# Layer 0 of a four-layer kernel: an outer level of 26 products for blocks of 4 by 4 by 2 in place of 7 for 2 by 2 by 2

## The chip, the cores and the metric

One core of one Trainium2 chip. The metric is the device time of one launch in microseconds, the median of several runs. Engines are named as in the profile: PE (TensorE, matmuls), PEld (its weight loads), DVE (VectorE), ACT (ScalarE), POOL (GpSimd) and SP (SyncE, here a queue of DMAs). POOL also issues DMAs, among them all that add to what lies in memory.

## What is computed

The input x has 1024 images of 16 by 16 by 16 values, in float32. Four layers follow, each `x = x + layer(norm(x))` with a group norm over 8 groups. Layers 1 and 3 are cellular-automaton steps (two depthwise convolutions, a dense layer to 128, a dense layer to 16, a mask), layer 2 is a 3 by 3 convolution. This case is about layer 0, cut here to what matters:

```python
def _tt_matvec(vector, cores):        # cores: (1,16,16,16), (16,16,16,16), (16,16,16,1)
    res, bs = vector[:, None], vector.shape[0]
    for core in cores:
        r, o, i, k = core.shape
        res_t = res.reshape(bs, r, i, -1)
        new = jnp.einsum('roik,brix->bkox', core, res_t)
        ...
x = x + _tt_matvec(_gn(x), (core0, core1, core2))
```

So layer 0 is one matrix of 4096 by 4096, given by three small cores, times a matrix of 4096 by 1024 (the images as columns).

## The kernel before

Layer 0 is worked as a dense product with two levels of Strassen's scheme. The outer level cuts the matrix in 2 by 2 blocks and the images in two chunks of 512 (`xf[0]`, `xf[1]`): 7 products (the table `OUTER`) take the place of 8. The inner level (`INNER`) does the same for each of these products, with 256 images at a time. One outer product is a phase. A phase has 8 units (output lines `q` of 4, `w` of 2), a unit 7 inner products of 8 matmuls of 128x128 by 128x256 (`pieces`, L1299), in 14 pieces of 4 matmuls. Each inner product sums its 8 matmuls in half a PSUM bank; `gather` (L1337, L1343, L1345, L1347) adds the bank to the result tile `r` of the unit.

The weights are never stored whole. `train_setup` makes g, the product of the last two cores, and puts it in `g_dram`. For each unit `gload` (L1216) brings two tiles of g from there, and `build` (L1229, copied out by L1231) multiplies them with `R`, the small matrix of the first core with the signs of this outer product, made by `coefs`. `R` mixes two rows of lines of g, so a build makes the weights of any combination of the outer blocks that lie in those rows. `mix` (L1256, L1258) adds the blocks for the inner products on DVE.

The operand of a phase is 4096/2 rows by 512 images and lies in one of two big tiles `XN[p % 2]`. While a phase runs, `part_steps` loads the next operand's blocks into the other (L1059), with a second block by pieces of 512 KB in the work buffers `t4` (L1084) that are added (L1095), and `combined` (L1039) makes three more sums. `centre_scale` (L1010) applies the norm to a block at its first use; the normed block is kept in memory (`xb`). `store` (L1281, L1283) sends the finished `r` of a unit to one or two blocks of `xf`: the first time by a plain DMA of SP, and then by an accumulating DMA of POOL (512 KB each). The work buffers are `r` with two and `t4` with three buffers; three PSUM banks hold products (`o`), four the builds (`w`), one other things (`m`).

The order on each engine is written out by hand. `run(layer, us, loads, *spans)` emits the pieces of a phase one after the other, and between them other steps: each span is a list of steps with costs, spread over a part of the phase. So beside phase 0 lie the second half of the first chunk's input (transposes, L925) and the weight folds of layer 1 (`make1`; PE L390, POOL DMAs L402); beside phase 1 the input of the second chunk (loads by POOL, L907, statistics on DVE, L919, transposes); beside phase 2 the folds of layer 3; beside phases 3 and 4 the residual (16 accumulating DMAs for each chunk, L1141); at the start of phase 4 the conv weights of layer 2 (POOL DMAs L438, L446, L449); beside phase 6 the norm for layer 1.

The diff's functions and the loops that call them:

Of the kernel before, what the change touches and what calls it, by code (L numbers as in the profile page):

```python
# [2 lines left out]

# [17 lines left out]
P = 128  # L21
# [83 lines left out]
def conv_preact_kernel(ctx: ExitStack, tc: tile.TileContext, a: dict, out: bass.AP):  # L105
# [99 lines left out]
    al_d = cst("al_d", [P, 1])  # L205
    V.tensor_tensor(al_d, al_c[:, 0:1], al_c[:, 1:2], ALU.subtract)
# [16 lines left out]
    def nca_weights(pre, room):  # L223
# [7 lines left out]
        flat = room.rearrange("p n b -> p (n b)")  # L231

        def tmp(rows, line, lo, n):
            return flat[0:rows, NB * line + lo : NB * line + lo + n]

        fc0n, fc1n = tmp(HID, 0, 0, 48), tmp(16, 0, 64, HID)
        ones, cb, b0 = tmp(16, 0, 192, 48), tmp(48, 0, 240, 1), tmp(HID, 0, 241, 1)
        fc0t, fcb = tmp(16, 1, 0, 3 * HID), tmp(48, 2, 0, 3 * HID)
        ind = tmp(48, 3, 0, 768).rearrange("p (s r) -> p s r", s=3)

        fs = tmp(P, 5, 0, NB)
        tk4 = tmp(P, 6, 0, 32 * len(TERMS)).rearrange("p (n c) -> p n c", c=32)

        tc3 = tmp(96, 2, 384, 96).rearrange("p (j k) -> p j k", k=3)
        tk = tmp(96, 9, 0, 32 * len(TERMS)).rearrange("p (n c) -> p n c", c=32)
        tp = tmp(P, 14, 0, 72 * len(TERMS)).rearrange("p (n f m) -> p n f m", f=2, m=36)
        pk = tmp(P, 10, 0, 833)
        fold_e = [tmp(P, line, 0, 2 * NB) for line in (12, 7, 3)]
        zero = tmp(32, 0, 256, HID)
# [171 lines left out]
    def conv_weights():  # L421
# [44 lines left out]
    g_dram = dram.tile([2, 4, P, 2, 4, P], F32, tag="g_dram", name="g_dram")  # L466

    xb = {
        (b, n): dram.tile([P, S, NB], F32, tag=f"xb{b}{n}", name=f"xb{b}{n}")
        for b in range(2)  # L470
# [4 lines left out]
        ([(0, 0, 1)], {(1, 0): 1, (1, 1): -1}),  # L475
        ([(1, 0, 1), (0, 0, -1)], {(0, 0): 1, (1, 0): 1}),
        ([(1, 1, 1)], {(0, 1): 1, (0, 0): -1}),
        ([(0, 0, 1), (1, 1, 1)], {(0, 0): 1, (1, 1): 1}),
        ([(1, 0, 1), (1, 1, 1)], {(0, 0): 1}),
        ([(0, 1, 1), (1, 1, -1)], {(0, 1): 1, (1, 1): 1}),  # L480
        ([(0, 0, 1), (0, 1, 1)], {(1, 1): 1}),
    ]
    INNER = [
# [16 lines left out]
    def part_lines(p):  # L500
# [3 lines left out]
    mr = [  # L504
        XN[n].rearrange("p n b -> p (n b)")[:, 14336:15360].rearrange("p (k i) -> p k i", k=2)
        for n in range(NCH)
    ]
# [5 lines left out]
    def train_setup(room, kept_room):  # L513
# [4 lines left out]
        c1t = kept_room.rearrange("p (h x m) -> p h x m", h=2, x=4)  # L518
# [25 lines left out]
        def sums():  # L544

            t = st0["A"] = work([P, 3, P], "A", "A")
            pt = bank([P, 2, P], "o", "pc0")
            for e in range(2):
                T.transpose(pt[:, e], c0r[:, e].rearrange("p n k -> p (n k)"), ident)
            pt = pt.rearrange("p e (o b i) -> p b i e o", b=2, i=8)  # L550
            for b in range(2):
                A.copy(t[:, b].rearrange("p (i e o) -> p i e o", e=2, o=8), pt[:, b])
            V.tensor_tensor(t[:, 2], t[:, 0], t[:, 1], ALU.add)

        def cores():
# [4 lines left out]
            for h in range(2):  # L560
                pt = bank([P, 4, P], "o", "pc1")
                for x in range(4):
                    T.transpose(pt[:, x], c1s[:, h, x].rearrange("p r k -> p (r k)"), ident)
                A.copy(c1t[:, h], pt)

        def gmul(pg, h, ih, x, r, q):
            rows = slice(32 * r, 32 * r + 16)
            T.matmul(
                pg, c1t[rows, h, 2 * ih + x], c2[rows, 64 * q : 64 * q + 64], start=True, stop=True
            )  # L570

        def early():
# [3 lines left out]
            for x in range(2):  # L576
                for hi in range(4):
                    for r in range(4):
                        gmul(pg[r][:, x, hi], hi // 2, hi % 2, x, r, 0)
# [7 lines left out]
            for h in (1, 0):  # L587
                G.dma_start(
                    g_dram[h, 0].rearrange("p i o f -> p i (o f)"),
                    g[:, 2 * h : 2 * h + 2].rearrange("p i o f -> p i (o f)"),  # L590
                )

        def piece(q, h, r0):
# [20 lines left out]

        rest = [
            (0.6, lambda q=q, h=h, r0=r0: piece(q, h, r0))
            for q in range(1, 4) for h in range(2) for r0 in (0, 2)
        ]
        return sums, cores, early, rest

# [273 lines left out]
    def input_steps(n, tag, queue):  # L897
# [4 lines left out]
        slots = XN[1 - n].rearrange("p n b -> p (n b)").rearrange("p (s f) -> p s f", s=8)  # L902
        X = part_lines(0)

        def load(half, bg):
            b0 = n * NB + bg * P
            queue.dma_start(  # L907
                slots[:, 4 * half + bg],
# [3 lines left out]
        def stats(half, bg):  # L912
# [4 lines left out]
            x = slots[:, 4 * half + bg].rearrange("p (q g i) -> p q g i", g=8, i=2)  # L917
# [3 lines left out]
        def turn(h, wh):  # L921
            pt = bank([P, 4, P], tag[0], "ptin")
            for bg in range(4):
                x = slots[:, 4 * (h // 8) + bg].rearrange("p (h w f) -> p h w f", h=8, w=2)
                T.transpose(pt[:, bg], x[:, h % 8, wh], ident)  # L925
            pt = pt.rearrange("p g b -> p (g b)")
            if n == 0 and h < 8:
                if h >= 4:
                    A.copy(X[:, 1, 4 * wh + h - 4], pt)
                else:  # L930
                    A.copy(raw[:, 4 * wh + h], pt.rearrange("p (n i) -> p n i", n=2))
# [46 lines left out]
        def kept(b):  # L978
            for wh in range(2):
                to = xr[n][wh, 4 * b : 4 * b + 4]  # L980
                if b:
                    G.dma_start(to.rearrange("h p b -> p h b"), X[:, 1, 4 * wh : 4 * wh + 4])
                    continue
                for i in range(2):
                    G.dma_start(
                        to.rearrange("h p (n b) -> p h n b", n=2)[:, :, i],
                        raw[:, 4 * wh : 4 * wh + 4, i],
                    )
# [7 lines left out]
                for b in (2 * half, 2 * half + 1)  # L996
                for wh in range(2)
                for h in range(4 * b, 4 * b + 4)
# [44 lines left out]
    def raw_piece(b, n, l, k):  # L1043

        return xr[n][l // 4 % 2, 8 * b + 4 * (l // 8) + l % 4 : 8 * b + 4 * (l // 8) + l % 4 + k].rearrange(
            "h p b -> p h b"
        )

    full = slice(0, NB)

    def part_steps(p):


        blocks = OUTER[p][0]
        L = part_lines(p).rearrange("p b t i -> p (b t) i")
        b, n, _ = blocks[0]
        fresh = (b, n) not in made
        steps = [
            (0, lambda l=l: nc.sync.dma_start(  # L1059
                L[:, l : l + 4], raw_piece(b, n, l, 4) if fresh else xb[b, n][:, l : l + 4]  # L1060
            ))
            for l in range(0, 16, 4)
        ] + [8]
        if fresh:
            made.add((b, n))
            for l in range(0, 16, 2):
                x = L[:, l : l + 2]
                steps += [(1.2, lambda x=x, k=k: centre_scale(x, x, n, full, k)) for k in range(2)]
                if l % 4 == 2:
                    steps.append((0, lambda l=l: nc.sync.dma_start(  # L1070
                        xb[b, n][:, l - 2 : l + 2], L[:, l - 2 : l + 2]
                    )))
        if p == 1:
            return steps + from_first() + combined(p)
        if len(blocks) > 1:
            b1, n1, sign = blocks[1]
            fresh1 = (b1, n1) not in made
            made.add((b1, n1))
            t = {}

            def fetch(l):
                if l < 16:
# [841 lines left out]
```

## Time and profile before

| what | value |
|---|---|
| median of 3 runs | 2842.35 us (2841.89 to 2847.46) |
| the profiled execution | 2848.94 us, span 2847.2 us |
| granted PE clock, mean | 0.987 |
| PE busy | 2781.9 us, 98% |
| DVE, ACT, POOL busy | 1666.2, 1232.6, 452.2 us |
| layer 0 (40 to 1650 us): PE, DVE, ACT, POOL busy | 1597.22, 795.99, 419.15, 294.46 us |
| product matmuls of layer 0 (L1299) | 6272 records, 1426.3 us |
| builds (L1229) | 3584 records, 137.2 us |
| accumulating stores of `r` (L1283, from r and neg) | 64 |

How to read it: a float32 matmul has two records. "Busy" is the time in which at least one instruction of the engine runs; the matmuls overlap in the pipeline, so that a record of 384 ns takes 227 ns of busy time on average. The windows view gives the busy time by stretches, the chain of waits what ended last, and a wait in the timeline stands in brackets with what ended it.

### The profile page before, as it was taken

The page shows a single profiled execution, that of the slowest core. Times are in us where ns is not written, and L with a number is a line of the kernel's source. Part 1 is how long each engine was busy: PE and PEld are TensorE (multiplying, and loading weights), DVE is VectorE, ACT ScalarE, POOL GpSimd, SP SyncE. Part 2 cuts the span into 40 slices and gives each one's busy share as a digit, 9 for nine tenths or more (in the row PEclk, how much of TensorE's full clock was granted, in tenths as well). Part 3 has the DMA queues.
Part 4 walks back from the last instruction along what each step waited for, and adds up shares of the span by engine and source line. Part 5 has one row for each costly group of instructions (what it writes and reads, how often), then busy time and mean ns, then how long its engine had stood idle before and what let it go on. Part 6 is the DMA issues. An engine that isn't in the chain of part 4 may idle for free.

```text
span 2847.2 us, 47308 instructions
## 1 busy us (share of the span) xinstructions
PE 2781.9 (98%) x19028; PEld 1827.0 (64%) x19028; DVE 1666.2 (59%) x2196; ACT 1232.6 (43%) x2168; POOL 452.2 (16%) x661
## 2 busy tenths in 40 slices
PE   7999999999999999999999999999999999999997
PEld 5878888877888888888888843333333333334343
DVE  8426645633544345434456668757877877766654
ACT  3352232233221111211222256676778666666664
POOL 2351000263012131001000001101112221110000
PEclk7999999999999999999999999999999999999998
DMA  6276636366486477363261145546566866444665
GB/s 232 85 163 216 229 114 175 80 107 162 115 202 117 99 153 175 67 173 62 55 172 34 27 140 114 107 108 165 111 147 137 206 100 184 102 93 105 178 174 203
DMA packets 250188, 383.41 MB, mean 135 GB/s; under 512 B 30293, under 2 KB 140425, under 8 KB 243825
## 3 DMA queue, kind: packets, MB, share of 16 engines
q1 hardware_dynamic: 187344, 262.36, 28.7%
q0 software_dynamic: 62432, 117.88, 25.5%
q8 instruction: 151, 2.47, 0.4%
q14 instruction: 69, 0.56, 0.1%
q10 hardware_dynamic: 192, 0.13, 0.0%
HBM read 211.31 MB, written 173.92 MB: 135 GB/s over the span
## 4 chain that ended last, share of the span: by engine, by line
PE 73%; DVE 4%; issue 3%; DMA 2%; POOL 1%; ACT 1%; SPq 0%; DVEq 0%; POOLq 0%; ACTq 0%
PE po L1299 37%; PE ph L1708 17%; PE po L1537 7%; PE po L1392 5%; PE pw L1229 3%; PE po L1401 1%; DMA xn<-xf 1%; PE ptx L1601 1%; DVE xn L677 1%; DVE u L1549 1%; DMA convn<-in_L_conv_filters_dram 0%; PE pcnt L1577 0%; PE L_conv_pe L390 0%; PE pr L824 0%; DMA xf<-r 0%
## 5 line engine op out<-in xcount | busy, mean ns | idle before, releaser
L1299 PE MATMUL po<-xn,s 128*128 128x256 f32 x3584 | 815.3, 384 | 6.5 <-ACT r L1345 3.4
L1711 ACT ACTIVATE hid<-ph,pack 128x512 f32<-128x512 f32 (+1 forms) x1040 | 641.0, 684 | 324.2 <-PE ph L1708 260.4
L1299 PEld LDWEIGHTS po<-xn,s 128*128 128x128 f32 x3584 | 679.8, 192 | 115.3 <-issue 7.0
L1299 PE MATMUL po<-xn,w 128*128 128x256 f32 x2688 | 611.0, 382 | 0.0
L1299 PEld LDWEIGHTS po<-xn,w 128*128 128x128 f32 x2688 | 502.8, 190 | 84.8 <-issue 13.6
L1708 PE MATMUL ph<-xn,wq 32*128 32x512 f32 (+1 forms) x3752 | 516.8, 591 | 4.0 <-DVE u L1549 3.6
L1231 ACT COPY w<-pw 128x512 f32<-128x512 f32 x448 | 230.0, 601 | 513.6 <-PE pw L1229 314.2
L1708 PEld LDWEIGHTS ph<-xn,wq 32*128 32x128 f32 x3752 | 234.2, 185 | 229.5 <-issue 208.6
L1256 DVE TENSOR_TENSOR s<-w 128x1024 f32<-128x1024 f32 x224 | 271.1, 1220 | 182.2 <-PE po L1299 181.8
L1708 PE MATMUL ph<-xn,pack 32*128 32x512 f32 x1288 | 281.4, 620 | 7.6 <-DVE u L1549 5.3
L1337 DVE TENSOR_TENSOR r<-r,po 128x512 f32<-128x512 f32 x168 | 115.2, 686 | 281.6 <-PE po L1299 253.9
L1537 PE MATMUL po<-hid,pack 128*32 128x512 f32 (+1 forms) x2080 | 261.4, 596 | 0.7 <-ACT hid L1711 0.5
L1343 ACT COPY r<-po 128x256 f32<-128x256 f32 x112 | 41.6, 372 | 459.6 <-PE po L1299 431.7
L1347 DVE TENSOR_TENSOR r<-r,po 128x256 f32<-128x256 f32 x112 | 47.1, 420 | 328.8 <-PE po L1299 328.8
L1283 POOL DMA_DIRECT2D xf<-r x56 | 68.8, 1374 | 944.7 <-DVE r L1337 500.4
L677 DVE TENSOR_TENSOR xn<-xn,m 128x1024 f32<-128x1024 f32 x160 | 188.3, 1217 | 36.9 <-ACT m L700 36.9
L1549 DVE SCALAR_TENSOR_TENSOR u<-po,pack,xn 128x512 f32<-128x512 f32 (+1 forms) x130 | 96.3, 741 | 158.6 <-PE po L1537 157.5
L1591 POOL DMA_DIRECT2D xf<-u x96 | 82.6, 861 | 640.2 <-DVE u L1589 618.8
L1708 PEld LDWEIGHTS ph<-xn,pack 32*128 32x128 f32 x1288 | 117.8, 188 | 95.7 <-issue 69.5
L1537 PEld LDWEIGHTS po<-hid,pack 128*32 128x32 f32 x2080 | 54.7, 109 | 179.4 <-ACT hid L1711 85.1
L1392 PE MATMUL po<-xn,convw 128*128 128x512 f32 x368 | 163.6, 598 | 0.0
L1229 PE MATMUL pw<-R,gq 32*128 32x128 f32 x3584 | 137.2, 286 | 6.5 <-DMA gq<-g_dram 6.2
(190 smaller groups left out, 2337.7 us busy)
## 6 DMA issues: line engine op xcount, KB each, us to landing
xn<-xf SPq DMA_DIRECT2D x96, 512.0 KB, 7.2
wq<-L_conv_wy SPq DMA_DIRECT2D x192, 192.0 KB, 2.8
xf<-r POOLq DMA_DIRECT2D x56, 512.0 KB, 7.1
gq<-g_dram SPq DMA_DIRECT2D x440, 64.0 KB, 2.9
xf<-u POOLq DMA_DIRECT2D x96, 256.0 KB, 4.2
piece<-xb SPq DMA_DIRECT2D x32, 512.0 KB, 4.8
xf<-xr POOLq DMA_DIRECT2D x32, 512.0 KB, 11.6
xf<-conv POOLq DMA_DIRECT2D x64, 256.0 KB, 5.7
```

Source lines behind the costliest of these rows:

```text
L677: V.tensor_tensor(part, part, m().unsqueeze(1).broadcast_to([P, 2, NB]), op)
L1229: T.matmul(pw[r][:, v, i], g[rows, 2 * v + i], R[rows], start=True, stop=True)
L1231: A.copy(w.rearrange("p i b t m -> p (i b t) m")[:, :, 32 * r : 32 * r + 32].rearrange("p k (v o) -> p v k o", v=2), pw[r].rearrange("p v ...
L1256: V.tensor_tensor(t.rearrange("p i t m -> p i (t m)"), x, y, f)
L1299: T.matmul(po, matrix(u, what)[:, i, t], x, start=i == t == 0, stop=i == 1 and t == 3)
L1337: V.tensor_tensor(part, part, po.unsqueeze(1).broadcast_to([P, 2, 256]), ALU.add)
L1392: T.matmul(st["po", h][wh], conv["fw"][:, y], X[:, 16 * wh + h + y - 1], start=y == max(0, 1 - h), stop=y == min(2, S - h),)
L1537: T.matmul(po[32 * j : 32 * j + 32], nca["w1"][:, v], hid[j], start=v == 0, stop=v == 1)
L1549: V.scalar_tensor_tensor(u, po, nca["b1"], X[:, 8 * q + w2, cols(hf)], ALU.add, ALU.add)
L1591: G.dma_start(tile_cw(xf[n], 8 * q + w2), u, accum_op=ALU.add)
L1708: T.matmul(ph, w, x, start=k == 0, stop=k == len(tiles) - 1)
L1711: A.activation(h, ph, AF.Relu, bias=nca["bt"][:, r : r + 1])
```

## The change

The outer level is now a scheme of 26 products for blocks of 4 (output) by 4 (input) by 2 (chunks of images). A product has half the rows of one before. Two products that use the same lines of g are done together as a pair, so that a build makes weights for both; there are 13 pairs, and a pair is a phase of 4 units. A unit does the seven inner products for both products of its pair: of the 8 matmuls of a piece pair, 4 go to one half of a PSUM bank for the first product and 4 to the other half for the second. The table gives for each pair the lines of g, a step that joins the two results before they are stored, and for each product the combination of weight blocks, of operand blocks (four quarter blocks by two chunks) and of outputs.

```diff
     OUTER = [
-        ([(0, 0, 1)], {(1, 0): 1, (1, 1): -1}),
-        ([(1, 0, 1), (0, 0, -1)], {(0, 0): 1, (1, 0): 1}),
...
+        ((0, 2), None, ("-... .... .... ....", "+00", "-00 +01"),
+            (".--. .... .--. ....", "+10", "-00 +10")),
+        ((1, 3), (1, 0, 1), (".... .... .... ..++", "+20 -10", "-20 +30 +21 -31"),
+            (".... -... .... +...", "+30 +00 -20", "+30")),
...
+        ((0, 2), None, ("..+. .... .++. ....", "+10 -20 -21", "-00 +10 +20 -21 +31"),
+            ("..+. .... .... ....", "+21", "-00 +10 +20 +01 -11 -21")),
...
+        ((0, 1, 2, 3), None, ("..-. ..-- .--. ....", "+20 +21", "+00 -10 -20"),
+            ("..+. +.+. .... -..+", "+30 -20", "-10 +11")),
...
-        units = [(ph, q, w) for ph in range(7) for q in range(4) for w in range(2)]
+        units = [(j, q) for j in range(NP) for q in range(4)]
...
-                        T.matmul(pw[r][:, v, i], g[rows, 2 * v + i], R[rows], start=True, stop=True)
+                    for k, g in enumerate(gs):
+                        for r in range(4):
+                            rows = slice(32 * r, 32 * r + 32)
+                            T.matmul(
+                                pw[r][:, v, i], g[rows, 2 * v + i], R[rows, k],
+                                start=k == 0, stop=k == len(gs) - 1,
+                            )
...
-                    T.matmul(
-                        po, matrix(u, what)[:, i, t], x, start=i == t == 0, stop=i == 1 and t == 3
-                    )
+                    T.matmul(po[:, i], matrix(u, what)[:, i, t], x, start=t == 0, stop=t == 3)
...
+                    gload(u + 1, 1, 2)
...
+                    gload(u + 2, 0, 2)
...
+            if inner:
+                x, y, sign = inner
+                V.tensor_tensor(r[x], r[x], r[y], ALU.add if sign > 0 else ALU.subtract)
...
-                part = r[:, lo : hi + 1 : hi - lo]
-                V.tensor_tensor(part, part, po.unsqueeze(1).broadcast_to([P, 2, 256]), ALU.add)
+                part = r[:, :, lo : hi + 1 : hi - lo]
+                V.tensor_tensor(part, part, po.unsqueeze(2).broadcast_to([P, 2, 2, 256]), ALU.add)
```

What else goes with it:

- `gload` brings a tile by 4 DMAs of 32 rows where its two lines lie side by side in `g_dram`, and else by 8 of 16 rows; the three pairs with more than two lines have a second tile, in a single buffer at the end of `XN[1]`, loaded after pieces 6 and 11 of a unit (`gload(u + 1, 1, 2)`, `gload(u + 2, 0, 2)`). The line 4 stands for the sum of lines 0 and 1; `both` makes it in phase 1 and keeps it as a third part of `g_dram`.
- `coefs` writes `R` in halves of 64 columns from the four quarter blocks of the first core.
- `store` joins results on DVE, negates on ACT or combines on DVE into tiles of `t4`, and has 2 to 7 targets in a unit where it had 1 or 2.
- `part_steps` makes two operands of half the size, from up to four blocks each; a block that both use is loaded once.
- `r` has one work buffer; from the fifth unit on every second unit has its `r` at the end of `XN[0]`.
- The steps beside the phases are spread anew over 13 phases of 107 us: `make1` beside phase 3, `make3` beside phase 5, the conv weights at the start of phase 7, the residual beside phases 4 and 6 to 10, the second chunk's input beside phase 1 with `both`, the norm for layer 1 beside phase 12, and the making of the rest of g (`piece`) within phase 0.

## The prediction

> **What bounds the kernel now.** First the page's engine totals, then the slices, the stages by windows, the chain of waits, and last what each engine waits for.
>
> ```profile
> PE 2781.9 (98%) x19028; PEld 1827.0 (64%) x19028; DVE 1666.2 (59%) x2196; ACT 1232.6 (43%) x2168; POOL 452.2 (16%) x661
> ```
>
> PE (TensorE) is never free. The windows of layer 0, one row for each of its seven phases (columns: stretch; its length, then busy PE, PEld, DVE, ACT and POOL with instruction counts; granted clock, DMA share, GB/s):
>
> ```profile
> 40.00:308.00 268.00, 261.55 (x1767) 210.31 (x1768) 150.71 (x182) 93.03 (x215) 81.34 (x159) 0.96 0.52 147
> 540.00:774.00 234.00, 232.60 (x1506) 188.00 (x1505) 97.14 (x128) 74.21 (x148) 90.77 (x169) 0.99 0.52 115
> 774.00:990.00 216.00, 216.00 (x1418) 186.21 (x1418) 91.25 (x102) 44.45 (x97) 33.30 (x31) 1.00 0.65 138
> 990.00:1216.00 226.00, 222.62 (x1435) 191.51 (x1434) 110.80 (x123) 43.85 (x98) 48.09 (x68) 0.98 0.62 143
> 1216.00:1430.00 214.00, 214.00 (x1409) 184.47 (x1408) 90.26 (x99) 43.39 (x96) 19.37 (x16) 1.00 0.43 96
> ```
>
> PE idles 13 us in the 1610 us of the layer; DVE is half busy, DMA 31% to 65%. The chain of waits in a settled stretch is one unit of work, on PE alone:
>
> ```profile
> 714.20 17.46 PE po L1299 x80
> 731.66 1.10 PE pw L1229 x32
> 732.76 7.10 PE po L1299 x32
> 739.87 1.10 PE pw L1229 x32
> ```
>
> So a unit is 17.46 + 1.10 + 7.10 + 1.10 = 26.76 us, and 56 units are 1499 of the 1610 us; the rest is transposes, folds and start-up, which stay. The time is PE's work plus whatever makes PE wait.
>
> **PE's work.** A new unit has the same 56 matmuls (two records each) and the same two builds, but there are 13 pairs by 4 = 52: 4 x 26.76 = 107.0 us go. Three pairs (the 6th, 10th and 11th) use more than two lines of g, so each of their 12 units builds from two tiles: 2 x 12 more groups of 32 records, 24 x 1.10 = 26.4 us. Net -80.6 us. Everything below is how much of that is given back.
>
> **Vector work.** Before, a unit has 5 mixes at 1.22 us (L1256, L1258), 3 gathers of 512 at 0.69 (L1337) and 2 of 256 at 0.42 (L1347): 9.0 us. Now the two products don't share a bank, so the gathers are 1024 and 512 wide: 5 x 1.22 + 3 x 1.22 + 2 x 0.69 = 11.1 us, and `store` adds one to three instructions of 1.22. The operand of a phase has 4 adds (1.22 each) for every term beyond the first, up to 20, 8 normings for each fresh block, and 10 steps of `combined`, 12.2 us, all of it now inside 107 us and no longer 214. Summed over the instruction order, phases 1 to 11 hold 59 to 107 us of DVE work; PE has 107 to 134 us in them. Two places don't fit. In phase 0 the operand of phase 1 lies in units 2 and 3: 2 x 11.1 + 2 x 1.2 (stores) + 16 normings, 4 adds, 12 of `from_first` and 10 of `combined` (42 x 1.22 = 51.2) = 75.8 us, against PE's 2 x 26.8 and five pieces of g (80 of 256 records at 18.7 us in all: 5.8), 59.4 us. It is in order, so +16 us. In the last phase units 1 to 3 hold 90.9 us of DVE against 3 x 26.8 plus some 7 of statistics: +4 us. Bounds: 8 to 30 and 0 to 14. ACT gets 4 copies of 0.60 for 4 of 0.38 a unit, some 1 us in 26.8, hidden: it is a fifth to a third busy.
>
> **DMA.** Stores to xf grow from 96 transfers of 512 KB to 176; 32 were and are plain, the accumulating ones go from 64 to 144. Operand loads grow too. Prices from one window each of the DMA queues:
>
> ```profile
> DMA packets 19793, 29.83 MB, mean 138 GB/s; under 512 B 1728, under 2 KB 9920, under 8 KB 19268
> ...
> q0 software_dynamic: 8432, 16.25, 44.3%
> q1 hardware_dynamic: 11348, 13.38, 19.9%
> ```
>
> That is phase 3 of before: 44.3% of 216 us over 16.25 MB is 5.9 us of all sixteen engines for each accumulated MB (POOL's queue), 19.9% over 13.38 MB is 3.2 us for a plain MB (SP's). In phase 2 the POOL queue took 28.9% of 234 us = 68 us, of which 8 accumulating stores (4.2 MB) are 25, so one set of weight folds is 43. By these, new phase 3 (seven stores a unit, one of them plain in part, a fold, two blocks to load, one to save) needs 14.7 x 3.2 + 12.6 x 5.9 + 43 = 164 us, against PE's 107 + 18 for the fold (its windows: 232.6 - 214) = 125. Phase 4 needs 8.4 x 3.2 + 11.5 x 5.9 = 95 of 107, phase 5 14.7 x 3.2 + 8.4 x 5.9 + 43 = 140 of 134 (with the doubled builds); the others 55 to 100 of 107 to 126. The excess of phase 3 is 39 us; a store may be a unit late (its `r` is needed again two units on, and three PSUM banks give 7 us more) and phase 4 takes up 12. I take half, +20; phase 5 +6. Bounds: 0 (all of it drains later) and the full excess plus DVE's waits on late pieces, 45 together for phase 3 and 20 for phase 5.
>
> **Waits it adds.** In the three pairs with two tiles, the second tile has one buffer: its load for the second build is queued when the first build has read it, and the next build stands four pieces, 7.1 us, later; behind it on PE is everything. A load is eight DMAs in two of these pairs; SP's issue of one took 0.60 us (median) and up to 0.97 in the stretch at 727 us, landing 3.0 median: 8 x 0.6 + 3.0 = 7.8, 0.7 us too late, for 8 units: +6 us. Bounds 0 and 8 x (7.8 + 4.7 - 7.1) = 43. `r` has one buffer through phase 0: a gather on ACT waits for the stores to land, 3.2 us on SP's queue after some 4 us, and PE reaches the bank 10.5 us on: nothing. Steps with nothing to pay: the re-ordered lines, `kept`, the tile places, the moved conv weights (27 us of POOL's queue ahead of one store, as before).
>
> **What a long wait costs.** One such wait is in the trace, PE's rows around it:
>
> ```profile
> 1026.11 1.17 PE L1229 MATMUL pw<-R,gq 32*128 32x128 f32 x32
> 1030.67 10.03 PE L1299 MATMUL po<-xn,s 128*128 128x256 f32 x32 [3.38 <-ACT r L1345]
> 1040.64 1.17 PE L1229 MATMUL pw<-R,gq 32*128 32x128 f32 x32
> 1041.74 7.17 PE L1299 MATMUL po<-xn,w 128*128 128x256 f32 x32
> ```
>
> ACT waited for a POOL store queued behind the conv weights; PE stood 3.38 us, and the 32 records after it took 10.03, not 7.10: 2.9 us more, at a granted clock of 0.50. Of the stalls above I expect three as long: +8 us. The Trainium skill ("TensorE: Matmul & The Clock Gate", Part 1: The HAM clock gate) says that the clock halves after an idle window of about 3.4 us and comes back after one busy window; an estimate from it is 1.7 us for each stall, 5 in all. It speaks against this change, which trades a steady PE for one that waits, and the row here is dearer than the rule.
>
> **The sum.** -80.6 + 16 + 4 + 20 + 6 + 6 + 8 = -20.6 us. The profiled execution took 2848.94 us (span 2847.2, 1.7 around it); 2828.3. The median of the runs, 2842.35, lies 6.6 below that execution: 2822 us.
>
> **Rivals.**
> 1. *The accumulating stores set the end: slower.* Place: phases 3 to 5 and 8. Price: DMA work of layer 0 goes from about 824 us (the shares by windows) by 42 MB x 5.9 and 50 MB x 3.2, 408 us, to 1230 of some 1550. If the pieces of an operand land in 11.6 us, as the residual's transfers do in the busy phase 3 of before, and not in 4.8, DVE loses some 3.5 us for each of 60 pieces, 210 us, where DVE's free time in these phases is about 150: 60 more on PE. -20.6 + 60 = +39: 2882. It decides from 81 us of stalls in all. For it: the share of 0.65 becomes over 0.8, with 1.3 in phase 3. Against: at 0.65 DVE waited 1.1 us in all for pieces, since SP runs ahead by three buffers.
> 2. *DVE is the bound in the crowded phases.* In phases 3, 5, 6 and 12 a unit has 25 to 32 us of DVE work; if each of 16 units costs 1.5 us for the order within it, +24: 2846, no change to be seen. Against: DVE's waits are for PE almost alone (329 and 254 us for the gathers), and 26.4 still fits 26.8.
> 3. *Nearly all stalls are absorbed.* Only phase 0 and the last cost, 8 to 20 us: 2770 to 2782. For it: before, the DMA share of 0.65 cost PE nothing (216.00 of 216.00).
> 4. *The work isn't saved.* Excluded almost: the order of instructions has 224 matmuls of 128x256 in each of 13 phases, 2912 for 3136, and 384 more builds. Only if the matmuls ran longer with two halves of a bank as targets; nothing suggests it: 2%.
>
> **How the numbers follow.** The forecast (stalls of 35 to 75 us, 2797 to 2837) 0.37, absorbed 0.18, no visible change (within 0.2%, 5.7 us, about what a measurement of this kernel can tell from no change: stalls of 75 to 87) 0.10 with the DVE rival in it, slower 0.35, nearly all the DMA rival. Faster 0.55. Cases of both signs hold the most, so: the forecast's own range is 2797 to 2837. The 8-in-10 range leaves out one in ten at each end: 2770, where only phase 0 costs, and 2885, just past the DMA rival's price.
>
> **What would show it.** After: 5824 records of the product matmuls at an unchanged 0.218 us start to start; units of 26.8 us where nothing is late, 29 in the three pairs. Phase 0's second half with PE waiting for DVE. In phase 3 a DMA share near 1.0 and PE waiting behind ACT or DVE that wait for xf stores or pieces; in phases 5 and 10 short PE waits for gq. I am wrong if PE idles over 81 us more in the layer, or if phase 3 runs at 125 us.

## The result and the profile after

The kernel became slower: 3015.09 us (median of 4 runs, 3012.74 to 3022.03) against 2844.9 for the kernel before on the same chips, a ratio of 1.0602 with a 95% interval of 1.0579 to 1.0625. The profiled execution has a span of 3011.0 us, 163.8 more than before's, at a mean granted clock of 0.957 (0.987 before). The forecast was 2822, its range ended at 2885.

PE's line of the page, to be held against the one shown of before (98%):

```profile
PE 2778.6 (92%) x19092; PEld 1809.1 (60%) x19092; DVE 1994.1 (66%) x2422; ACT 1267.9 (42%) x2132; POOL 559.3 (19%) x738
```

PE is busy for the same time, in a longer span, and DVE for 328 us more. The whole of layer 0 by the windows view, in the columns of the prediction's windows; the first fence is before, the second after:

```profile
45.00:1645.00 1600.00, 1591.13 (x10402) 1336.65 (x10402) 786.60 (x985) 415.49 (x889) 293.25 (x464) 0.99 0.51 125
```

```profile
45.00:1810.00 1765.00, 1588.77 (x10466) 1317.03 (x10466) 1111.81 (x1205) 449.83 (x853) 402.57 (x546) 0.94 0.68 167
```

These two rows hold the accounts. PE's idle time goes from 1600 - 1591.1 = 9 us to 1765 - 1588.8 = 176: 167 more. Its busy time should have fallen by the 80.6 us of the prediction to 1510.5 and is 1588.8: 78 us more, because the granted clock is 0.94 and no longer 0.99, so that the same matmuls run longer. -80.6 + 167 + 78 = +164, the difference of the spans. The records are those foretold: 3328 + 2496 = 5824 product matmuls.

Six of the 13 phases, by windows (phases 0, 1, 3, 5, 6 and 12):

```profile
45.00:210.00 165.00, 141.73 (x960) 117.49 (x960) 115.89 (x107) 42.70 (x112) 1.17 (x3) 0.90 0.47 167
210.00:375.00 165.00, 135.88 (x840) 112.92 (x840) 87.32 (x171) 47.41 (x86) 3.08 (x6) 0.93 0.62 225
...
490.00:675.00 185.00, 139.99 (x804) 103.89 (x803) 97.84 (x113) 53.11 (x98) 108.64 (x179) 0.84 0.82 167
...
795.00:982.00 187.00, 154.00 (x999) 116.44 (x999) 97.39 (x114) 52.79 (x97) 106.38 (x174) 0.85 0.73 151
982.00:1089.00 107.00, 107.00 (x705) 92.20 (x704) 91.52 (x87) 26.17 (x49) 17.93 (x16) 1.00 0.82 197
...
1672.00:1810.00 138.00, 119.55 (x655) 94.39 (x653) 105.37 (x112) 36.71 (x59) 11.01 (x9) 0.95 0.44 108
```

Phase 6 is the kernel as forecast: 107 us, PE busy in all of them, at full clock, with DVE at 91.5 of 107 and a DMA share of 0.82. Phases 3 and 5 stand beside it with the same or a lower DMA share, and take 185 and 187 us. What differs most is POOL's count, just left of the clock: 179 and 174 instructions (the weight folds), and 16 in phase 6. Set each phase against an estimate of PE's own work in it (107 us, more by what the phase adds on PE: transposes in phases 0 and 1, a fold's 18, double builds' 9, statistics), and the lengths in us are:

| phase | 0 | 1 | 2 | 3 | 4 | 5 | 6 | 7 | 8 | 9 | 10 | 11 | 12 |
|---|---|---|---|---|---|---|---|---|---|---|---|---|---|
| after | 164 | 165 | 116 | 185 | 120 | 187 | 107 | 108 | 117 | 134 | 116 | 107 | 138 |
| PE's own work | 131 | 126 | 107 | 125 | 107 | 134 | 107 | 107 | 107 | 116 | 116 | 107 | 114 |
| over it | 33 | 39 | 9 | 60 | 13 | 53 | 0 | 1 | 10 | 18 | 0 | 0 | 24 |

The five phases beside which a large piece of other work lies (input and g, the second chunk's input and the sum of two lines, two folds, the norm) hold 209 of the 260 us. Before, the same pieces lay beside phases of 214 us, and PE idled 9 us in the whole layer.

What PE waited for, from the waits view (us in total, times, longest):

```profile
PE pw L1369 <- DMA xn<-g_dram: 32.0, 22, 7.3
PE ptin L992 <- ACT lines L1002: 27.6, 16, 6.0
PE L_conv_pe L392 <- ACT xn L398: 26.7, 2, 23.4
PE pw L1369 <- ACT xn L398: 18.3, 3, 11.6
PE L_conv_pe L392 <- POOL xn L350: 11.2, 2, 6.7
```

The five rows are 116 of the layer's 176 us: the second g tile, the transposes of the input, and three for the folds (L392 to L398), 56 us between them. DVE's gathers (L1503) end one wait of a product, of 0.2 us, and a store of `xf` none. Those stand one step back. The waits of the other engines in phase 3:

```profile
ACT xn L398 <- DMA L_conv_wy<-xn: 58.8, 4, 35.3
DVE xn L1142 <- DMA piece<-xb: 53.2, 5, 23.8
...
SPq L1444 <- ACT neg L1428: 48.0, 3, 28.3
```

ACT's fold copies (L398) refill a buffer once its send (L404) has left, and the sends lie in POOL's queue among the accumulating stores; ACT works in order, so behind a waiting L398 lie the copies of the builds and the gathers. On SP the plain stores (L1444) wait for ACT's negation, and behind them lie the loads of pieces, for which DVE then waits. PE's end of this chain, in the timeline of phase 3:

```profile
593.88 2.32 PE L392 MATMUL L_conv_pe<-xn 9*36 9x512 f32 x8 [23.40 <-ACT xn L398]
...
634.32 2.55 PE L1369 MATMUL pw<-xn,gq 32*128 32x128 f32 x28 [11.57 <-ACT xn L398]
```

Two waits make 35 of the 45 us for which PE stood in this phase. In phase 5, which holds the other fold, half of PE's 33 us of waiting is for the second tile of g:

```profile
PE pw L1369 <- DMA xn<-g_dram: 16.5, 8, 7.3
PE pw L1369 <- ACT xn L398: 6.1, 1, 6.1
PE L_conv_pe L392 <- POOL xn L350: 4.5, 1, 4.5
PE L_conv_pe L392 <- ACT xn L398: 3.3, 1, 3.3
```

### The profile page after: what moved, and what is told of

Same layout as the page of the kernel before. It is cut to its first block, busy times and chain, and to the rows that moved or that the text cites. A ratio compares the mean times of both kernels' runs of the same rounds, so it can differ in the third digit from the quotient of the medians.

```text
span 3011.0 us, 48408 instructions
## 1 busy us (share of the span) xinstructions
PE 2778.6 (92%) x19092; PEld 1809.1 (60%) x19092; DVE 1994.1 (66%) x2422; ACT 1267.9 (42%) x2132; POOL 559.3 (19%) x738
## 3 DMA queue, kind: packets, MB, share of 16 engines
q1 hardware_dynamic: 210960, 314.82, 32.9%
## 4 chain that ended last, share of the span: by engine, by line
PE 67%; DMA 13%; DVE 9%; POOL 4%; issue 4%; ACT 2%; SPq 1%; DVEq 0%; ACTq 0%; POOLq 0%
PE po L1465 27%; PE ph L1874 19%; PE po L1703 7%; PE po L1558 5%; PE pw L1369 4%; DMA xf<-neg 3%; DMA L_conv_wy<-xn 2%; DMA xn<-g_dram 2%; POOL L_conv_wy L404 2%; DVE xn L741 1%; PE po L1567 1%; DMA xr<-lines 1%; DMA xf<-r 1%; DMA xf<-xr 1%; DVE xn L1074 1%
## 5 line engine op out<-in xcount | busy, mean ns | idle before, releaser
L1465 PE MATMUL po<-xn,s 128*128 128x256 f32 x3328 | 772.1, 390 | 22.7 <-DVE s L1399 10.5
L1465 PEld LDWEIGHTS po<-xn,s 128*128 128x128 f32 x3328 | 640.2, 195 | 136.2 <-issue 26.7
L1465 PE MATMUL po<-xn,w 128*128 128x256 f32 x2496 | 592.3, 394 | 9.8 <-DVE w L1401 4.8
L1465 PEld LDWEIGHTS po<-xn,w 128*128 128x128 f32 x2496 | 485.7, 197 | 100.7 <-issue 13.1
L1399 DVE TENSOR_TENSOR s<-w 128x1024 f32<-128x1024 f32 x208 | 251.2, 1218 | 61.4 <-PE po L1465 60.9
L1142 DVE TENSOR_TENSOR xn<-xn,piece 128x1024 f32<-128x1024 f32 x96 | 116.7, 1219 | 128.2 <-DMA piece<-xb 128.1
L1103 DVE TENSOR_TENSOR xn<-xn 128x1024 f32<-128x1024 f32 x130 | 156.3, 1217 | 14.7 <-DMA xn<-xb 14.7
L1503 DVE TENSOR_TENSOR r<-r,po 128x1024 f32<-128x1024 f32 x84 | 102.3, 1218 | 93.6 <-PE po L1465 52.7
L1369 PE MATMUL pw<-xn,gq 32*128 32x128 f32 x2816 | 133.6, 295 | 18.3 <-ACT xn L398 18.3
L1503 DVE TENSOR_TENSOR xn<-xn,po 128x1024 f32<-128x1024 f32 x72 | 87.6, 1217 | 84.8 <-PE po L1465 62.4
```

Source lines behind the costliest of these rows:

```text
L1103: V.tensor_tensor(out, y, z, f)
L1142: V.tensor_tensor(y, y, x(), ALU.add if sign > 0 else ALU.subtract)
L1369: T.matmul(pw[r][:, v, i], g[rows, 2 * v + i], R[rows, k], start=k == 0, stop=k == len(gs) - 1,)
L1399: V.tensor_tensor(t.rearrange("p s t m -> p (s t m)"), x, y, f)
L1465: T.matmul(po[:, i], matrix(u, what)[:, i, t], x, start=t == 0, stop=t == 3)
L1503: V.tensor_tensor(part, part, po.unsqueeze(2).broadcast_to([P, 2, 2, 256]), ALU.add)
```

## The experiments

Theory A was that the folds' sends, caught in POOL's queue among the accumulating stores, are what stops PE. Theory B was that the traffic of the stores does, and theory D, which came after the first runs, that each piece of side work costs what it costs because it now has half to two thirds of the time, whatever lies in the queues. "Phase n: a to b" compares with the table above.

**The sends on another queue.** In `send` (L404):

```diff
-                            G.dma_start(
+                            nc.sync.dma_start(
```

> The weight folds' 80 sends each (48 KB) are queued on SP and not on POOL; same bytes, same order otherwise. Theory A (queue order: the sends stand behind accumulating stores in POOL's one queue, ACT's copies of the next fold wait for their buffer, PE waits for ACT): phases 3 and 5 fall from 185 and 187 us to some 140 each, 2920 to 2940 us in all. Theory B (the sixteen DMA engines are full in phase 3, 164 us of work for 125 us, whichever queue holds it): phase 3 stays within 10 us of 185, and the whole within 20 us of 3015.

3011.49, ratio 1.0569 (1.0538 to 1.0599). Phase 3: 185 to 172; phase 5: 187 to 195. POOL's queue alone isn't it: DVE still waited 53.4 us for pieces in phase 3, now behind the sends on SP, and PE 22.9 us for DVE; in phase 5 PE once waited 20.8 us for a second tile of g. Theory A falls as it was put, since phase 3 should have come to some 140; the wait changes its place. That the folds' sends and the other transfers hold each other up, in whichever queue they share, is not excluded by this run: SP's queue has its own loads and stores. Theory B's bound for the total held, its bound for phase 3 (10 us) was missed by 3.

**Without the accumulating stores.** The 144 stores are left out (L1442):

```diff
-                    G.dma_start(to, have[c], accum_op=ALU.add)
+                    pass
```

> Leaves out the 144 accumulating stores of layer 0 (xf then holds only the first plain stores and the residual). Theories A and B both take the fold phases down to 125 to 140 us. It prices the stores as a whole: if the DMA rival of the prediction carries the loss, about 261 us of excess falls to the share of phases 0, 1 and 12, some 95 us: 2850 us. If the loss has other causes, over 2900.

2916.08, ratio 1.0234 (1.0201 to 1.0267): some 105 us less by the ratios. Phase 3 goes to 154, phase 5 to 156.5; phases 0, 1 and 12 stay at 159.5, 164 and 140.5. So the stores have a part, but a kernel that accumulates nothing is still 2.3% slower than before. PE's waits in it:

```profile
PE ptin L992 <- ACT lines L1002: 24.9, 16, 6.0
PE L_conv_pe L392 <- POOL xn L350: 11.2, 2, 6.5
```

The long wait behind L398 is gone. The folds' other wait stays at 11.2 us: it is for POOL's own steps of the fold, and the stores have no part in it.

**Without the folds.** `make1` and `make3` are left out; two plain DMAs fill the tensors from other data.

```diff
-                fold = {3: make1, 5: make3}.get(j)
+                fold = None
+                filled = {3: L1, 5: L3}.get(j)
+                if filled:
+                    fill(filled)
```

> Leaves out both weight folds: the tensors that they fill get other finite data by two plain transfers at the start of phases 3 and 5, so the later layers compute with wrong weights at the same cost. Stores stay. If folds and stores together are what phases 3 and 5 can't hold, both drop to 110 to 120 us (PE's folds, 18 us, are gone too): 3015 - 135 = 2880. If the stores alone saturate DMA, phase 3 stays above 140.

2931.35, ratio 1.0287 (1.0241 to 1.0334), some 90 us less, of which the folds' own work on PE is 36. Phase 3 goes to 132.5, phase 5 to 137.5, between the two cases expected. In phase 3, then, the stores without folds cost 25 us over PE's work, the folds without stores 29, and both together 60. PE's rows there show the price of a wait:

```profile
516.21 10.13 PE L1465 MATMUL po<-xn,s 128*128 128x256 f32 x32 [3.11 <-DVE s L1399]
```

3.11 us of waiting, then 10.13 for 32 records that take 7.10 elsewhere: 6.1 us in all.

**Without the sum of lines 0 and 1.** `both` is left out; pair 2 reads line 0 in its place.

```diff
-                where = [(2, 0) if l == 4 else (l % 2, l // 2) for l in pair]
+                where = [(0, 0) if l == 4 else (l % 2, l // 2) for l in pair]
...
-            (part_steps(2) + combined(2), 0.78, 1.0), (both, 0.1, 0.9),
+            (part_steps(2) + combined(2), 0.78, 1.0),
```

> Leaves out the sum of g's lines 0 and 1 (8 loads, 4 adds, 4 writes in phase 1); builds of line 4 read line 0 in its place, so values differ and the work is the same. Theory: in phase 1 the sum's tiles hold two of the three t4 buffers, the transposed lines wait for the third and PE's transposes for ACT (21 us of PE waits seen): phase 1 falls from 165 to some 145, 2995 in all. Rival: phase 1 is held by the statistics on DVE and the input loads, and stays at 160 to 165.

2982.15, ratio 1.0466 (1.0435 to 1.0496). Phase 1: 165 to 144, and PE's wait there for the transposed lines (L992 for L1002) falls from 21.0 to 9.6 us. Half of what phase 1 is over its work comes from this step, which the prediction never priced.

**Four DMAs for a tile of g in the four-line pairs.** With the lines in another order, two and two lie side by side.

```diff
-        ((0, 1, 2, 3), None, ("..-. ..-- .--. ....", "+20 +21", "+00 -10 -20"),
+        ((0, 2, 1, 3), None, ("..-. ..-- .--. ....", "+20 +21", "+00 -10 -20"),
```

> The two pairs with four lines take them in the order 0, 2, 1, 3, so that each tile's two lines lie side by side and a tile comes by 4 DMAs and not 8; same bytes, same builds. Theory: the second tile is late because SP needs 8 x 0.59 us to issue it; PE's 32 us of waits for it fall by half to three quarters, phase 5 by 10 to 20 us, 2990 to 3000 in all. Rival (the transfers themselves are late, DMA being full): within 8 us of 3013.

2986.51, ratio 1.0502 (1.0442 to 1.0562). PE's waits for g fall from 32.0 to 17.7 us (in phase 5 from 16.5 to 8.4), and phase 5 from 187 to 174. Phase 9 falls from 134 to 125, though its tiles come as before; why is not shown.

**A place of its own for the third unit's `r`**, in the part of the big tile that phase 0 does not use:

```diff
-                    if k == 0 and (u < 4 or u % 2):
+                    if k == 0 and u == 2:
+                        st["r", u] = flats[1][:, 12288:14336].rearrange(
+                            "p (s a n) -> p s a n", s=2, a=2
+                        )
+                    elif k == 0 and (u < 4 or u % 2):
```

> The third unit's result tile gets a place of its own (the end of the next operand's sums, not yet used then), so that in phase 0 only the second unit waits for its predecessor's stores. Theory: the single r (33 us of ACT waits for xf stores) holds phase 0: from 164 to 145 to 152 us, 3000 in all. Rival: DVE's 76 us of work in two units of 59 us holds it: phase 0 stays at 160 to 164.

2997.22, ratio 1.054 (1.0397 to 1.0683). Phase 0: 164 to 158, though ACT's wait of 32.9 us for the stores of `r` (L1509) was there to be taken away.

**No sum for the next operand in phase 0** (`combined(1)`, ten DVE steps of 1.22 us, is left out):

```diff
-            steps_of(phases[0]), 107, (), (lines[1], 0.16, 0.45), (part_steps(1) + combined(1), 0.46, 1.0),
+            steps_of(phases[0]), 107, (), (lines[1], 0.16, 0.45), (part_steps(1), 0.46, 1.0),
```

> The changed kernel without the ten vector steps of phase 0 that make the sums of the next operand (12.2 us of DVE; phase 1 then reads old finite values in their place). If DVE's overload holds the end of phase 0, as the prediction says, phase 0 falls by 8 to 13 us, from 164 to some 153. If other waits hold it (the single r, the transposes), by less than 4.

3010.6, ratio 1.0605 (1.0562 to 1.0648); phase 0: 164 to 160, and phase 1 takes 170. Neither of the two edits seemed to matter much. Together they do:

**Both of these edits.**

> Two edits in phase 0 together: the third unit's r has a place of its own (as in the run that did only this, phase 0 went from 164 to 158 us), and combined(1), ten DVE steps of 1.22 us that make the operand of phase 1, is left out (as in the run that left out only this, 160 us). If both the wait of ACT for the stores of the one r and DVE's overload lie one behind the other, so that each hides the other when it is taken away alone, phase 0 falls by more than the two alone: to 142 to 150 us. If the rest of phase 0 is start-up work and transposes that neither edit touches, it stays at 153 to 156. The total: 2975 to 2995 in the first case, 2990 to 3005 in the second.

Phase 0: 164 to 144, 20 us, where the two alone gave 6 and 4. PE's waits in phase 0 of the kernel after and of this one:

```profile
PE pw L1369 <- ACT g L652: 6.8, 1, 6.8
...
PE po L1465 <- DVE xn L1103: 4.7, 2, 3.2
PE po L1465 <- ACT r L1511: 3.3, 1, 3.3
```

```profile
PE ptin L992 <- ACT lines L1002: 6.5, 3, 5.9
PE po L1469 <- DVE xn L1103: 2.8, 1, 2.8
PE po L1469 <- DVE xn L1074: 2.6, 1, 2.6
```

The waits behind ACT (the copy L652 of g and the gather L1511, both queued behind the gather that waits for the one `r`) are gone. With only the `r` given, DVE had been late in their place (PE then waited 5.9 us for L1399). The total didn't follow as expected: 3001.4 (2993.41 and 3009.39), ratio 1.0559 (1.0486 to 1.0631), and phase 1 grew from 165 to 171. How far single phases can be read: counted from the first product of phase 0 to the first of phase 1, it took 164 to 168 us in nine profiled runs that leave it as it is, 157 and 162 with one edit each, and 147 with both. So the 4 us of the one edit alone are hardly clear of that spread; the 20 are.

**The folds spread over four phases** (half of one in each of phases 3, 5, 7 and 9; the conv weights move to phase 10, and the folds' two small tables to tiles that are free until then):

```diff
-                fold = {3: make1, 5: make3}.get(j)
+                fold = {3: paused(make1)[:32], 5: paused(make1)[32:], 7: paused(make3)[:32], 9: paused(make3)[32:]}.get(j)
```

> Each weight fold is spread over two phases (layer 1: 3 and 5, layer 3: 7 and 9) by keeping its two source tiles in constants that are free then; the conv weights go to phase 10. Same work, half as dense. Theory A2 (density: fold sends and accumulating stores together exceed what queues and DMA can hold in one phase, so ACT's copies wait): phases 3 and 5 lose 30 to 45 us each, phases 7 and 9 gain 20 to 30 each: 2960 to 2990. Rival (any fold step beside these phases costs its waits, however spread): the sum of phases 3 to 10 stays within 15 us.

2976.9, ratio 1.0469 (1.0424 to 1.0514). Phase 3: 185 to 151, phase 5: 187 to 146, but phase 7: 108 to 136 and phase 9: 134 to 140. Of 75 us taken away, 34 come back in the two phases that take the other halves.

**All of the repairs together**: the lines' order, the third `r`, the spread folds, pair 2 from three lines with no sum of lines, and the last phase's load and norm started earlier.

```diff
-        ((3, 4), None, ("..++ ..++ .... ....", "+30", "+00 -20"),
+        ((0, 1, 3), None, ("..++ ..++ .... ....", "+30", "+00 -20"),
...
-                    steps_of(phases[j]), 107, load_cw(X0, xf[0]) + [put(L1)], (bg, 0.2, 1.0), by=0.3
+                    steps_of(phases[j]), 107, load_cw(X0, xf[0]) + [put(L1)], (bg, 0.1, 1.0), by=0.12
```

> All mends together: the orders of e6, the result tile of e7, the spread of e8, pair 2 from lines 0, 1 and 3 in place of the summed line (no sum in phase 1, four units with a double build), and in the last phase the layer's output loaded at once and the norm started earlier. If the causes are separate, the gains add: some 20 + 12 + 35 + 25 + 10 = 100 us, 2910. The kernel before, 2845 to 2849, is beaten only if the waits feed each other; I expect not.

2927.43, ratio 1.0295 (1.024 to 1.035), 17 us above what was expected. Half of the loss is repaired; before is not beaten.

**The same with the phases in another order**, so that pairs with few stores meet the folds (and the residual spread over phases 5 to 11):

```diff
-    OUTER = read(OUTER)
+    OUTER = [read(OUTER)[p] for p in (0, 1, 2, 6, 3, 10, 4, 7, 5, 9, 8, 11, 12)]
```

> The version c1 with the pairs in another order, so that the phases beside folds (3, 5, 7, 9) hold pairs of 2, 2, 3 and 3 stores a unit and the pair of 7 stores lies in phase 4, and with the residual spread over phases 5 to 11. Theory D: phases 3 and 7 lose 10 to 20 us more of their excess: 2895 to 2915. Rival (fold density alone): within 8 us of 2927.

2930.88, ratio 1.0309 (1.0281 to 1.0337): no gain. Phase 3 went from 152 to 116 with a pair of two stores, phase 4 from 119 to 141 with the pair of seven. PE's two largest waits in the layer:

```profile
PE pw L1368 <- DMA xn<-g_dram: 36.3, 20, 8.8
PE po L1468 <- DVE s L1398: 35.3, 10, 10.9
```

**The kernel before, with its side work squeezed.** This asks the question from the other end: the old products, and three pieces of side work in about the time that they have after the change: 0.63 of what they had for the second chunk's input, 0.64 for `make3`, 0.49 for the norm for layer 1.

```diff
-            ([(0, x) for x in loads] + [12] + woven_in + tail, 0.0, 0.6), (part_steps(2), 0.66, 0.97),
+            ([(0, x) for x in loads] + [12] + woven_in + tail, 0.0, 0.38), (part_steps(2), 0.66, 0.97),
...
-            steps_of(phases[2]), 210, (), (paused(make3), 0.02, 0.6), (part_steps(3), 0.62, 0.96),
+            steps_of(phases[2]), 210, (), (paused(make3), 0.02, 0.39), (part_steps(3), 0.62, 0.96),
...
-            steps_of(phases[6]), 210, load_cw(X0, xf[0]) + [put(L1)], (bg, 0.12, 0.97), by=0.2
+            steps_of(phases[6]), 210, load_cw(X0, xf[0]) + [put(L1)], (bg, 0.55, 0.97), by=0.2
```

> The kernel before with three steps beside its phases squeezed to the length they have after: the second chunk's input into 0.38 of phase 1, layer 3's weight fold into 0.37 of phase 2, the norm for layer 1 into the last 0.42 of phase 6; nothing added. Theory D (the loss is the density of steps that stayed as they were beside phases half as long): phases 1, 2 and 6 lose some 20 to 30 us each, 2905 to 2930. Rival (density alone is hidden; it takes the added vector work and stores): within 15 us of 2845.

2891.99 against 2842.96, ratio 1.0166 (1.0146 to 1.0186): +49 us with no work added. The three phases go from 232 to 240, 234 to 253 and 221 to 244, +8, +19 and +23.

**The kernel before, with more stores**: 80 accumulating and 16 plain ones of 512 KB, to tensors that nobody reads.

```diff
+            for n in range(2 if 1 <= ph <= 5 else 1):
+                to = side[n][2 * q + w].rearrange("w p b -> p w b")
+                if ph == n:
+                    nc.sync.dma_start(to, r)
+                else:
+                    G.dma_start(to, r, accum_op=ALU.add)
```

> The kernel before with 80 accumulating stores more (512 KB each, of the unit's result into memory that nothing reads), so 144 as after, and 16 plain ones; everything else as it was. Theory D: the accumulating traffic by itself is hidden in phases of 214 us (DMA share then 0.65 to 0.85): under 2865. Rival (the accumulating stores are the cause by themselves): 2900 or more.

2860.01, ratio 1.0055 (1.0036 to 1.0074): +17 us, at a DMA share of 0.66 in the layer (0.51 without them, 0.68 after the change). As many stores as the change adds are nearly hidden as long as the side work has room. They are not all that it adds: by GB/s and time the layer moves some 200 MB before, 250 in this run and 295 after, and the further loads of operands were not tried alone.

**Both in the kernel before.**

> The kernel before with both the squeezed steps of b1 (+49 us) and the 80 more accumulating stores of b2 (+17). If the two only add: 2905 to 2915. If fold sends and stores in POOL's one queue feed each other, as phases 3 and 5 after suggest, phase 2 alone loses 15 us or more over the sum: 2925 to 2940.

2920.5 against 2839.28, ratio 1.0289 (1.0265 to 1.0314): +81, where the two alone make 66. The interaction is there, some 15 us, smaller than the second case expected, in which fold sends and stores feed each other. The phase of the squeezed fold goes from 253 to 272, where the stores alone take it from 234 to 242, and PE's longest wait in the layer is the one that the changed kernel showed, here in the old products (the names are those of this kernel; 12.2 us with the squeezing alone, 23.4 after the change):

```profile
PE L_conv_pe L391 <- ACT xn L397: 20.2, 1, 20.2
```

**No accumulating stores, no folds, no sum of lines**: the three omissions above in one kernel.

> The changed kernel without accumulating stores, without folds and without the sum of lines 0 and 1 (the three left-outs of e2, e3 and e4 in one). If the causes add and PE's saving is real, the layer takes 1504 - 37 for the folds' PE work + some 90 of excess in phases 0, 1 and 12 = 1557 us, 2805 in all, below the kernel before. If PE waits for other things as well, 2850 or more.

2853.15, ratio 1.0033 (1.0022 to 1.0045). It doesn't answer the question: with nothing in its queue to hold it, POOL issued the fills and the residual at once, and they ran beside phase 1 (174 us, where 144 came without the sum alone).

**The same with POOL held to each phase** by a copy of one row of that phase's `R`:

```diff
-            spans = []
+            spans = [([lambda j=j: G.tensor_copy(come, st0["R", j][0:1, 0, 0:1])], 0.0, 0.01)]
```

> As e10 (no accumulating stores, no folds, no sum of lines 0 and 1), but with POOL held at the start of every phase from 2 on by a tiny copy that waits for that phase's R, so that the fills and the residual run in their own phases and not early beside phase 1, as e10's trace shows them to. If the causes add and PE's saving is real: phase 1 back to some 145 (e4), phase 2 to 112, the layer about 1555, 2805 to 2815 in all, 1% below the kernel before. If it stays at 2850, phases 1 and 2 are held by something else.

2810.27 against 2839.28, ratio 0.9901 (0.987 to 0.9932), as expected. The total alone would not show that the saving on PE is real, since the folds' 36 us on PE are missing here and not in the kernel before, and 29 is less. The phases show it: 3 and 6 to 8 take 107 to 110 us. By the ratios, the three omissions bring 105, 90 and 39 us alone, and 199 together, some 35 less than their sum, as it would be if some of the loss needs both stores and folds. Of the 199, 36 are the folds' own work; the other 163 are two thirds of the 167 us of waiting and 78 of longer work. Even so stripped, phases 0, 1 and 12 stand at 164, 142 and 140.

## Why the prediction was wrong

**Right: what PE is spared.** -80.6 us, 5824 records, units of 26.8 us: phases 6, 7 and 11 ran at 107 to 108 us in the full kernel, and 3 and 6 to 8 at 107 to 110 in the stripped one.

**Right: the load on the DMA queues, but not what follows from it.** Phase 3 was to need 164 us of all sixteen engines. Its queues:

```profile
q0 software_dynamic: 10090, 16.56, 55.8%
q1 hardware_dynamic: 8464, 14.16, 25.5%
```

81.3% of 185 us are 150, 14 less than was summed. The step that failed is the next: "I take half, +20; phase 5 +6", which treats the phase as a volume that drains late, for PE to catch up on. Measured: 60 and 53. The share of the sixteen engines over the phase doesn't decide (0.82 in phase 3, and 0.82 in phase 6, where PE waited for nothing). What stopped PE in phase 3 was single waits, of which 23.4 and 11.6 us were for a fold's copy on ACT, which itself stood behind a send; in phase 5 such waits are 9 of 33 us, and the second tile of g is 16.5. Of phase 3's 60, 29 came without any accumulating store and 25 without any fold.

**Wrong: side work that was moved cost nothing.** The prediction summed DVE's and DMA's totals for each phase and found room. It priced no chain of the side work (transposes on PE waiting for ACT's copies; statistics in sequence; folds from POOL to PE to ACT to POOL). Phase 1 was put at 0 and is 39 over, 21 of it the sum of lines; the last phase was put at +4 and is 24 over; phases 3 and 5 hold the folds. Squeezing alone, in the old kernel, gave +8, +19 and +23.

**Phase 0: the sum held, the cover didn't.** +16 for DVE was forecast, and "`r` has one buffer ... nothing". Phase 0 is 33 over. The two stand one behind the other in the same stretch: each removed alone gives 4 to 6 us, both 20. The failed step is the one `r`: the gather on ACT waited up to 13.9 us for its stores, and behind it in ACT's order were the copy of g and the next gather, for which PE stood 6.8 and 3.3 us. The prediction named who waits, and not what is queued behind that.

**The second tile of g: the wait was foreseen, its size and places not.** +6 was taken, from bounds of 0 to 43, for the 8 units whose second tile comes by eight DMAs (phases 5 and 10). PE waited 32.0 us for such tiles, 22 times: 16.5 in phase 5, where they took 5.4 us to land (median) and not the 3.0 of the sum; 1.8 in phase 10; 8.7 in phase 9, whose second tile comes by four DMAs and was put at nothing; and 5 at the ends of phases 4 and 8, for the phase that follows. The bound held. The formula, the same lateness in every one of the 8 units, did not: the four of phase 10 hardly waited.

**The clock: the mechanism was right and the number of waits wrong.** +8 was for three waits. 167 us of waiting came with 78 us of longer work at the lower clock, 0.47 us for each us waited. The Trainium skill ("TensorE: Matmul & The Clock Gate", Part 1: The HAM clock gate) says that the clock halves after an idle window of about 3.4 us. The rows here agree in kind, but a wait of 3.11 us already cost 3.0 more.

**The rivals.** The rival "the accumulating stores set the end" had the sign and one of the places, and a price of 2882; without any such store the kernel is still at a ratio of 1.0234. Its mechanism, DVE late because pieces are, is there: DVE waited 128.1 us for them in the layer, 24 times (1.1 before), though they landed in 5.7 us (median) and not 11.6, and in phase 3 without the folds PE's waits are for DVE's mixes, 14.9 us. "DVE is the bound" shows in phase 0, behind the one `r`; in phase 6, which it named, DVE was busy 91.5 of 107 us and PE waited for nothing. "Absorbed" is out. What came besides is a rival that was not written: the fixed side work in half to two thirds of the time. By itself, in the old kernel, it made 49 us, and 81 with the stores; the whole of what came after the change was not rebuilt there. The condition for being wrong was well put (over 81 us of idle PE; 167 came).

**Still open.** Phase 12 stands at 137 to 141 us in every variant that doesn't start its norm earlier; squeezing the norm in the old kernel cost the same 23 us. After the change PE waited 11.1 us in phase 12 for the sums of the norm (L876 for L716), but the load, the statistics and DVE's order in it were not separated. Nor is it shown which of the steps that phase 1 has beside it costs the other 18 us.

## What to carry to other kernels

When a kernel whose bound engine is 98% busy does less work, everything that was spread beside that work is compressed as well: list each chain of side work with its own length (engine to DMA to engine, each step's latency included), and compare that with the new, shorter cover, not only the sums by engine and queue. A wait on an in-order engine is priced by what is queued behind it, and two such waits in one stretch hide each other, so that removing either alone shows little. Ask of a saved microsecond on the bound engine whether it was also the cover of something; here 81 us saved came with 167 of waiting and 78 of longer work at a lower clock.

## What the hardware showed that was not expected

- A wait costs PE nearly half as much again: 0.47 us of longer work for each us waited, over the layer. How much depends on where the wait falls. 2.81 us before a group of 32 records in phase 1 were followed by 7.14 us, as without any wait; 2.17 us at the start of phase 1 of the run with both phase-0 edits by 8.83; 3.11 us in phase 3 of the run without folds by 10.13. The granted clock of these three traces tells why. In layer 0 it changes only on a grid of 3.41 us. All 72 intervals of the grid at full clock in which PE was busy for less than 0.42 of the time were followed by one at half clock, and 10 of the 1282 in which it was busy for more. The waits of 2.17 and 3.11 us leave an interval at 0.41 and 0.32; the wait of 2.81 us is split over two, at 0.67 and 0.50.
- A DMA of 32 KB to a tile of g took as long to issue on SP as one of 64 KB (medians of 0.59 and 0.60 us), so that eight half-size DMAs cost twice four.
- An accumulating store of 512 KB landed in a median of 7.1 us (longest 16.2) before, at a DMA share of 0.51 in the layer, and in 11.2 (27.4) after, at 0.68.
